# Graph message passing on one core: the sum of the last list of repeated rows stands one item behind the last unit of grouped sums

## The chip, the cores and the metric

The kernel runs on 1 core of one Trainium2 chip. The metric is the device time of one execution in microseconds (us). Before the change the median of 3 runs is 1887.07 us, with runs from 1877.03 to 1892.61.

## The reference, cut to what matters

There are 6250 nodes with 128 features and 200000 edges. Each edge takes the row of its `dst` node (normalised, through a ReLU and a matrix), multiplies it by a filter made from its 20 edge features, and adds the product to the row of its `src` node. The sums go through a small network and are added to `x`.

```python
idx_i, idx_j = pair_indices[0], pair_indices[1]          # src, dst; dst is sorted, src is random
x = atomic_embedding @ W_in                              # atomic_embedding = relu(layernorm(x))
W_ij = shifted_softplus(f_ij @ W_f1 + b_f1) @ W_f2 + b_f2
W_ij = W_ij * f_ij_cutoff
x_ij = x[idx_j] * W_ij
out = jax.ops.segment_sum(x_ij, idx_i, num_segments=N_ATOMS)
return shifted_softplus(out @ W_o1 + b_o1) @ W_o2 + b_o2  # and x + this
```

The part that matters here is `segment_sum`: 200000 rows of 128 numbers, each to be added to one of 6250 rows.

## The kernel before, in words

**Items.** The edges are cut into chunks of 128 and into 391 quads of four chunks. One loop (`for i in range(...)` near the end of the main block) runs over items `i`; at item `i` quad `i` is begun, and quads `i-1` to `i-4` are in later stages. Around these stages the loop runs hooks: `at(i, point, fn, ...)` registers a function for an item and a point in it, and `put(name, i, fn, ...)` does the same with the offset and the point that the table `AT` gives for a name. The points of an item are run in the order L, D0, D1, PE0, ..., A0, A1, AX, DM, DR, PE1, PE2, A2, D2, S. The whole loop is written under a manual schedule, so that each engine's instructions stand in the order in which the loop calls them. Nothing waits for an item as such: every engine runs on through its own queue until an instruction waits for data or for a free buffer.

**Three ways for a row to reach its sum.** The rows of an edge are added in one of three ways, by quad.

- *Plain* quads (the first 12 of those that are not grouped, and quad 390): rows of one chunk with the same `src` are summed by a matrix of equal ids (`s3_pe`), then scattered.
- *Listed* quads (184 of them, in 12 lists of at most 16 quads): the rows are scattered as they are. A scatter (`scatter`, L644) is an indirect DMA that GpSimd issues; it adds 128 rows to one of four accumulators in DRAM, `acc0` to `acc3`, in turn. A row whose `src` has occurred already within its chunk is sent to a row of the list's own region at the end of the accumulators, 128 rows per list. When a list is complete, `l_load` (L513) brings its region from all four accumulators into `lm`; `l_dg`, `over_row` (L807) and `l_same` (L525) compare the ids of its 128 rows with each other; `l_sum` (L531, L532) adds rows of equal id by matmul, over the four copies; `l_copy` (L537), `l_ji` (L542, L543) and `over_int` (L834) make the rows and their indices; and `over_scatter` scatters them into the nodes' rows.
- *Grouped* quads (194: every second one, from 2 to 388): their rows are sorted into slots of node groups by matmul (`permute`) and moved into `mst` by DMA (`regroup`). Eight quads (ten in the last round) make a round, and each round has four *units* of grouped sums. A unit (`unit_pe`, L863) is 96 matmuls, 120 in the last round, into four PSUM tiles `un`, against one-hot matrices that DVE builds (`unit_oh`, L845); `unit_evac` (L879) adds the four tiles to the accumulator `accT` in SBUF. Rows for which a group has no slot left are the *overflow*: for each pair of quads they are summed by `over_row`, `over_eq`, `over_sum` (L818 to L820), `over_copy`, `over_ji` (L830) and `over_int` and are scattered too.

**The end of the loop.** `unit_slots` puts the last round's units at items 395, 397, 399 and 401 (units 0 to 3 in what follows); each eviction stands at the point DM of the next item. The last quad's scatters stand at 394, and so does the overflow of quad 384; that of quad 388 has its sum at 396, its copy at 397, its indices at 398 and 399 and its scatter at 399. The loads of `x` for the output (L1202, L1207) stand at 395 to 399 on SyncE, and DVE adds a bias to them (L1212) at 398 to 407.

**The last list.** For list `w` the code takes the item `i` behind its last quad at which no unit stands: `clear(n, units)` counts `n` up until it is not an item of `units`. The last list ends with quad 389 and has a lag of 5, so that `i` is 394. From it follow: `l_start`, `l_dg` (ScalarE) and `over_row` (TensorE) at 394; `l_same` (DVE) at 395; `l_sum` at the first item from 395 without a unit, 396, at the point PE1, so between unit 0 (395) and unit 1 (397); `l_load` (SyncE) at 395; `l_copy` and `l_ji` at 397; `over_int` and the scatter at 400. The loads of a list wait for the scatters of listed rows, since these may write into its region.

**Buffers that this touches.** `un`, the overflow's sum and row, and the list's row and sum share the PSUM tag "B" with four buffers. The copies of overflow sums and list sums share the tag `os` with six buffers; a buffer is free again when its scatter has been done.

**After the loop.** The scalars of a check (L1418 to L1436) decide whether a slow second pass is needed; it isn't here, but the loop around it makes all engines meet at L1436, when the accumulators' scatters have landed and `accT` is complete. Then the *tail* loads the accumulators (`t_load`, L1521), adds them to `accT`, runs the two output layers and writes the result. `acc0` is read early; the tail reads the other three.

Of the kernel before, what the change touches and what calls it, by code (L numbers as in the profile page):

```python
# [75 lines left out]
def tile_gnn(ctx: ExitStack, tc: tile.TileContext, x, fB, cT, srcT, srcr, srci, dstr, win_, wf1, wf2, bias, bo1c, wo1,  # L76
# [28 lines left out]
    uslots = unit_slots(rounds)  # L105
    units = {i for us in uslots for i in us}
# [13 lines left out]
    NW = -(-(LE - LB) // SW)  # L120
# [3 lines left out]
    wend = [splain[LB + SW * w + wsize[w] - 1] for w in range(NW)]  # L124
    wlag = [LLAG] * (NW - 1) + [LASTLAG]
# [801 lines left out]
    with tc.manual_schedule():  # L927
# [126 lines left out]
        def at(i, point, fn, *a):  # L1054
            hooks.setdefault((i, point), []).append((fn, a))

        def put(name, base, fn, *a, busy=()):
            d, point = AT[name]
            i = max(clear(base + d, busy) if busy else base + d, 0)
            at(i, point, fn, *a)  # L1060
            return i
# [6 lines left out]
        if CE < EP // P:  # L1068
            w = (CE + 4 * NS) // 2
# [169 lines left out]
        for g in range(len(tgroups)):  # L1239
            i = clear(max(r0_at + 1, ret_at + 12), units)  # L1240
# [4 lines left out]
        for r in range(-(-len(mpq) // RKQ)):  # L1245
            i = mpq[RKQ * r]
            early = i < 8
            i = max(i, 4)
# [13 lines left out]
        for w in range(NW):  # L1262
            for g in range(wsize[w] // 4):
                n = LB + SW * (w - 1) + 4 * g - LSHIFT
                i = splain[n] + 2 if w else 6 + 2 * g
                while w and (i not in mpi or i in units):
                    i -= 1
                for k in range(2):
                    kk = (LB + SW * w + 4 * g) // 2 + k
                    at(max(0, i + k - 2), "L", sb_load, kk)  # L1270
                    put("l_eq", i + k, l_eq, kk)
                i = put("l_count", i, l_count, (LB + SW * w) // 4 + g, busy=units)
                k = put("l_dup", i, l_dup, w, g)
            i = put("l_scan", i, l_scan, w)
            i = put("l_before", i - 1, l_before, w, busy=units)
            put("l_index", i, l_index, w)
            assert i + 1 <= splain[LB + SW * w] + 1
            put("l_id", i, l_id, w)
            i = put("l_place", i, l_place, w, busy=units)
            put("l_take", i, l_take, w)  # L1280
            i = clear(wend[w] + wlag[w], units)
            at(i, "L", l_start, w)
            put("l_dg", i, l_dg, w)
            at(i, "PE2", over_row, ("L", w))
            put("l_same", i, l_same, w)
            k = clear(i + AT["l_sum"][0], units)
            at(k - 1, "L", l_load, w)
            at(k, AT["l_sum"][1], l_sum, w)
            put("l_copy", k, l_copy, w)
            put("l_ji", k, l_ji, w)  # L1290
            k = put("l_int", k, over_int, ("L", w))
            at(k, "S", over_scatter, ("L", w))
# [344 lines left out]
def unit_slots(rounds):  # L1637
    end = rounds[-1][-1]
    grouped = {q for qs in rounds for q in qs}
    out, used = [], set()  # L1640
    for r, qs in enumerate(rounds):
        a = qs[-1] + ULAG
        last = r == len(rounds) - 1
        step = 2 if last else min(RND // 2, (rounds[r + 1][-1] - qs[-1]) / 4)
        us = []
        for s in range(4):
            i = a + int(s * step)
            while i in used or (not last and i <= end and not UCLASSES[UCLASS](i, grouped)):
                i += 1
            used.add(i)  # L1650
            us.append(i)
        out.append(us)
    return out
# [10 lines left out]
def clear(i, busy, n=1):  # L1664
    while any(i + k in busy for k in range(n)):
        i += 1
    return i
# [114 lines left out]
```

## Time and profile before

| | us |
|---|---|
| median of 3 runs | 1887.07 |
| lowest and highest run | 1877.03, 1892.61 |
| the profiled execution | 1900.09 |
| its span, first to last instruction | 1898.3 |
| granted TensorE clock, mean over the span | 0.963 |
| unit 0 to unit 3 of the last round, in the trace | 1786.42 to 1845.91 |
| first load of the tail | 1849.09 |

The profile is one execution on the chip. PE is TensorE's matmul, PEld its weight load, DVE is VectorE, ACT is ScalarE, POOL is GpSimd, SP is SyncE; a "q" behind the name is the engine's sequencer or DMA queue. A timeline row has start, duration, engine, line, operation, output and inputs, how many instructions were merged, and in brackets the idle time before it with what ended it. A wait row has who waited, for what, the total, the number of times and the longest. A row of a stretch (A:B) has its length, then busy time and number of instructions of PE, PEld, DVE, ACT and POOL, the granted clock, the DMA engines' share and GB/s. Groups by line end with busy time, mean ns of one, and the idle time before them.

### The profile page before, as it was taken

Reading aid. Unit: us, or ns where it says so; the run is one execution under the profiler, and the core shown is the slowest. Engines: PE = TensorE matmul, PEld = TensorE weight load, DVE = VectorE, ACT = ScalarE, POOL = GpSimd, SP = SyncE. Lnnn points to the kernel's source line nnn. Section 1 sums busy time; section 2 is a strip of 40 time slices with the busy share of each in tenths; the row PEclk is TensorE's granted clock in tenths of the full one; section 3 lists DMA queues with packets and bytes.
Section 4 is the critical chain, followed back from the end, with each engine's and each line's share of the span. In section 5 each row is a group of like instructions: output and inputs, shape, how many; then the busy total and the mean of one; then the engine's idle time right before and its main releaser. Section 6 shows DMA issues by size and latency. Waiting matters only on the chain. (4 is left out here: it accounts for less than half of the span.)

```text
span 1898.3 us, 55497 instructions
## 1 busy us (share of the span) xinstructions
PE 1681.0 (89%) x19308; PEld 1122.6 (59%) x19308; DVE 1605.7 (85%) x4740; ACT 1471.1 (77%) x4068; POOL 1494.5 (79%) x949
## 2 busy tenths in 40 slices
PE   3769989999999999999999999999999999999746
PEld 2546655666666666666665566666666666666524
DVE  6678989899899989898899789889889899888636
ACT  4568878888788888887787788888888888888405
POOL 5557777888888888888888888888888888887845
PEclk8789999999999999999999999999999999999978
DMA  8878988888888888887887888888888888888647
GB/s 301 225 183 194 206 185 172 172 174 182 164 180 168 172 181 168 170 187 162 173 188 154 172 186 173 176 177 166 187 170 174 189 173 175 157 159 188 127 82 267
DMA packets 365471, 339.68 MB, mean 179 GB/s; under 512 B 86686, under 2 KB 328781, under 8 KB 365187
## 3 DMA queue, kind: packets, MB, share of 16 engines
q1 hardware_dynamic: 234005, 270.57, 49.1%
q0 software_dynamic: 130624, 65.33, 33.0%
q8 instruction: 152, 2.49, 0.6%
q14 instruction: 132, 1.08, 0.2%
q10 hardware_dynamic: 558, 0.20, 0.0%
HBM read 150.76 MB, written 108.08 MB: 136 GB/s over the span
## 5 line engine op out<-in xcount | busy, mean ns | idle before, releaser
L644 POOL DMA_INDIRECT acc<-s,lji x736 | 1188.0, 1614 | 245.1 <-issue 178.0
L572 ACT ACTIVATE xc<-xg,cb 128x128 f32<-128x128 f32 x1564 | 445.6, 371 | 16.9 <-PE xg L559 11.5
L567 PEld LDWEIGHTS W<-w,a 128*128 128x128 f32 x3128 | 428.7, 198 | 38.0 <-issue 24.7
L863 PE MATMUL un<-so,mst 32*128 32x392 bf16 x9312 | 433.9, 327 | 9.8 <-ACT sg L766 3.4
L567 PE MATMUL W<-w,a 128*128 128x128 f32 x3128 | 428.0, 281 | 0.1
L766 ACT CAST sg<-pq 128x388 bf16<-128x388 f32 x776 | 345.7, 493 | 84.6 <-DMA mst<-sg 45.4
L758 PE MATMUL pq<-pt,pm 128*128 128x388 bf16 x1552 | 333.4, 338 | 33.2 <-issue 9.1
L863 PEld LDWEIGHTS <-mst 32*128 32x128 bf16 x9312 | 232.8, 93 | 159.6 <-issue 19.0
L384 ACT ACTIVATE a<-a,con 128x512 f32<-128x512 f32 x391 | 282.4, 722 | 11.6
L379 ACT ACTIVATE a<-z 128x512 f32<-128x512 f32 x391 | 241.3, 617 | 39.1 <-PE z L374 34.1
L746 DVE TENSOR_TENSOR pt<-pt 128x512 f32<-128x512 f32 x388 | 264.1, 681 | 0.0
L879 DVE TENSOR_TENSOR accT<-un,accT 128x392 f32<-128x392 f32 x368 | 182.3, 557 | 68.0 <-PE z L374 42.5
L758 PEld LDWEIGHTS <-pm 128*128 128x128 bf16 x1552 | 147.3, 97 | 148.0 <-issue 58.0
L845 DVE TENSOR_SCALAR so<-iot,mst 128x392 bf16<-128x392 f16 x776 | 220.1, 334 | 8.6 <-PE un L863 7.1
L644 POOL DMA_INDIRECT acc<-os,oji x109 | 174.6, 1602 | 45.4 <-issue 17.0
L732 DVE TENSOR_SCALAR pm<-iotp,pos 128x384 bf16<-128x384 f16 x776 | 204.3, 324 | 0.0
L374 PE MATMUL z<-ft,ws 123*128 123x512 bf16 x391 | 155.0, 397 | 38.8 <-DMA ft<-fsd 11.1
L582 DVE TENSOR_TENSOR s<-W,xc 128x512 f32<-128x512 f32 x184 | 125.9, 684 | 70.7 <-issue 39.0
L582 DVE TENSOR_TENSOR pt<-W,xc 128x512 f32<-128x512 f32 x194 | 132.5, 683 | 47.4 <-ACT xc L572 31.0
L559 PE MATMUL xg<-wn,oh 63*128 63x128 bf16 x1564 | 157.1, 222 | 15.0 <-DVE oh L391 11.4
L556 PE MATMUL W<-b2rep,onesb 64*128 64x512 bf16 x391 | 154.5, 395 | 0.0
L781 PE MATMUL po<-pt,pm 128*128 128x387 bf16 x776 | 152.8, 338 | 1.3 <-DVE pt L746 0.7
(214 smaller groups left out, 1845.1 us busy)
## 6 DMA issues: line engine op xcount, KB each, us to landing
mst<-sg SPq DMA_DIRECT2D x776, 97.0 KB
sb<-src SPq DMA_DIRECT2D x98, 256.0 KB
rb<-reld SPq DMA_DIRECT2D x194, 128.0 KB
fsd<-f SPq DMA_DIRECT2D x49, 480.0 KB
ft<-fsd SPq DMA_DIRECT2D x96, 240.0 KB
fb<-in_fB_dram SPq DMA_DIRECT2D x49, 320.0 KB
ft<-fsd SPq DMA_DIRECT2D x96, 160.0 KB
acc<-s,lji POOLq DMA_INDIRECT x736
```

What stands on the lines that cost most here:

```text
L379: nc.scalar.activation(a, st[q]["z"], AF.Exp)
L384: nc.scalar.activation(a, a, AF.Ln, bias=half, scale=0.5)
L567: nc.tensor.matmul(W[:, c, :], st[q]["a"][:, c * P:(c + 1) * P], w2, start=False, stop=(c == 3))
L572: nc.scalar.mul(xc[:, c, :], st[q]["xg"][:, c, :], late["c", q // CQ][:, 4 * (q % CQ) + c:4 * (q % CQ) + c + 1])
L582: nc.vector.tensor_tensor(m[:, :, :P], st[q]["W"], st[q]["xc"], op=ALU.mult)
L644: nc.gpsimd.indirect_dma_start(out=accs[k][:rows, :], out_offset=bass.IndirectOffsetOnAxis(ap=ji, axis=0), in_=s, in_offset=None, compute_ ...
L732: nc.vector.tensor_scalar(pm[:, c], iotp, rk[r]["pos"][:, 4 * j + c:4 * j + c + 1], None, op0=ALU.is_equal)
L746: nc.vector.tensor_tensor(pt[:, :, k * P:(k + 1) * P], a, high(a), op=ALU.subtract)
L758: nc.tensor.matmul(t[:, :MW], mp[q]["pm"][:, c, s * P:(s + 1) * P], high(mp[q]["pt"][:, c:c + 1, :MW])[:, 0], start=(c == 2 * h), stop=(c ...
L766: nc.scalar.copy(mp[q]["sg", h][:, s], mp[q].pop(("q", k))[:, :MW])
L845: nc.vector.tensor_scalar(so, iotw[:, :GN], w[:, 3 * P // 2:3 * P // 2 + 1], None, op0=ALU.is_equal)
L863: nc.tensor.matmul(ts[g][:, :GN], mp[q]["ms", s // 2][v, s % 2, k * P:(k + 1) * P], mp[q]["oh"][v], start=(q == qs[0] and k == 0), stop=(q ...
```

## The change

The item at which the last list's operations start must lie behind the last unit of the last round as well. For all other lists the added term is 0 and nothing changes.

```diff
@@ -1278,7 +1278,7 @@
             put("l_id", i, l_id, w)
             i = put("l_place", i, l_place, w, busy=units)
             put("l_take", i, l_take, w)
-            i = clear(wend[w] + wlag[w], units)
+            i = clear(max(wend[w] + wlag[w], uslots[-1][-1] + 1 if w == NW - 1 else 0), units)
             at(i, "L", l_start, w)
             put("l_dg", i, l_dg, w)
             at(i, "PE2", over_row, ("L", w))
```

With `uslots[-1][-1]` = 401 the item `i` of the last list is 402 instead of 394. `l_start`, `l_dg` and `over_row` stand at 402; `l_load` at 402; `l_same` and `l_sum` at 403; `l_copy` and `l_ji` at 404; `over_int` and the scatter at 407. The loop runs to item 412 as before, and the number and order of the scatters are the same.

## The prediction

> **What bounds the kernel now.** The page came first: TensorE is busy for 89% of the span. The change touches only the end, so next came the waits there (TensorE's from 1790 to 1862 us, SyncE's from 1780) and then the timeline of each engine.
>
> ```profile
> span 1898.3 us, 55497 instructions
> PE 1681.0 (89%) x19308; PEld 1122.6 (59%) x19308; DVE 1605.7 (85%) x4740; ACT 1471.1 (77%) x4068; POOL 1494.5 (79%) x949
> ```
> ```profile
> PE lsum L531 <- DMA lm<-acc: 23.3, 1, 23.3
> ```
> ```profile
> SPq L513 <- DMA acc<-s,lji: 28.1, 1, 28.1
> SPq L1436 <- DVEq L1436: 14.0, 1, 14.0
> ```
>
> TensorE stands still once for 23.3 us, at the sum of the last list (L531), because its rows `lm` have not been loaded. They have not been loaded because SyncE held the load for 28.1 us until the last scatter into the list's rows (`s,lji`) had landed. TensorE's own timeline shows what is queued behind that sum:
>
> ```profile
> 1796.36 0.49 PE L531 MATMUL lsum<-lm,leq 128*128 128x128 f32 x2 [0.83 <-DVE accT L879]
> 1820.12 1.74 PE L531 MATMUL lsum<-lm,leq 128*128 128x128 f32 x6 [23.27 <-DMA lm<-acc]
> ...
> 1822.35 7.17 PE L863 MATMUL un<-so,mst 32*128 32x392 bf16 x120
> 1830.62 0.32 PE L863 MATMUL un<-so,mst 32*128 32x392 bf16 x1 [1.10 <-DVE accT L879]
> ...
> 1839.36 0.32 PE L863 MATMUL un<-so,mst 32*128 32x392 bf16 x1 [0.51 <-DVE accT L879]
> ...
> 1840.78 5.13 PE L863 MATMUL un<-so,mst 32*128 32x392 bf16 x117 [0.15 <-DVE accT L879]
> ```
>
> Three units of grouped sums follow the sum, from 1822.35 to 1845.91 (1840.78 + 5.13): 23.6 us of work that needs nothing of the list. GpSimd meanwhile works off a queue of scatters:
>
> ```profile
> 1798.08 1.54 POOL L644 DMA_INDIRECT acc<-os,oji  x1 [0.30 <-issue]
> ...
> 1807.31 1.54 POOL L644 DMA_INDIRECT acc<-os,oji  x1 [0.30 <-issue]
> ...
> 1814.69 1.54 POOL L644 DMA_INDIRECT acc<-s,lji  x1 [0.30 <-DMA acc<-s,lji]
> 1816.54 1.54 POOL L644 DMA_INDIRECT acc<-os,oji  x1 [0.30 <-issue]
> ...
> 1823.93 1.54 POOL L644 DMA_INDIRECT acc<-os,oji  x1 [0.30 <-issue]
> 1828.62 1.54 POOL L644 DMA_INDIRECT acc<-os,oji  x1 [3.15 <-ACT oji L834]
> 1830.47 1.54 POOL L644 DMA_INDIRECT acc<-os,oji  x1 [0.30 <-POOLq L1436]
> ```
>
> The last scatter is the list's own (1830.47), the one before it that of overflow 388. GpSimd ends at 1832.01, 14 us ahead of TensorE. The tail starts at the point where all engines meet (L1436); SyncE's 14.0 us there wait for DVE, and DVE for the last unit:
>
> ```profile
> 1845.80 1.98 DVE L879 TENSOR_TENSOR accT<-un,accT 128x392 f32<-128x392 f32 x4 [2.95 <-PE un L863]
> 1847.70 0.68 DVE L1212 TENSOR_TENSOR xl<-xl,bo2b 128x512 f32<-128x512 f32 x1
> ```
> ```profile
> 1848.56 0.02 SPq L1436
> ...
> 1849.09 0.38 SPq L1521
> ```
>
> So this stretch is bound by TensorE's queue, delayed by GpSimd's. The tail's first load leaves at 1849.09, and 49.2 us later the span ends; I take the tail as unchanged and forecast that one time.
>
> **The change part by part.** Work is neither added nor dropped. The last list's items move from 394 to 402 (start, diagonal, row), 395 to 402 or 403 (loads, comparison), 396 to 403 (sum), 397 to 404 (copy, index) and 400 to 407 (integer index, scatter). They move past units 1 to 3 on TensorE, their evictions on DVE, overflow 388's steps, and on SyncE past the loads of x, seven of which stood behind the held load. The order on GpSimd stays as it was: 388, then the list.
>
> *What goes from the old place.* DVE's evictions of units 0 and 1, and the list's index between them:
>
> ```profile
> 1795.74 1.98 DVE L879 TENSOR_TENSOR accT<-un,accT 128x392 f32<-128x392 f32 x4 [1.50 <-PE un L863]
> ...
> 1822.41 0.22 DVE L543 SCALAR_TENSOR_TENSOR ojd<-os,con,ojd 128x1 f32<-128x1 f32 x1 [23.64 <-issue]
> ...
> 1830.00 1.98 DVE L879 TENSOR_TENSOR accT<-un,accT 128x392 f32<-128x392 f32 x4 [1.98 <-PE un L863]
> ```
>
> Overflow 388's sum takes the list's place on TensorE at about 1796.4, and unit 1 starts when the eviction of unit 0 (1795.74) has freed its tiles. Unit 2 started 0.6 us after its predecessor's eviction began (1830.62 after 1830.00); with 388's tile to fill first I allow 1.3, so unit 1 starts at 1797.0 instead of 1822.35, 25.35 us earlier. DVE, which the list's index held for 23.6 us, is let go too. With the 23.56 us that the units took, unit 3 would end at 1820.6. The moved loads of x cost nothing on the path: their rows are read by DVE's additions (L1212) only beside or after the units.
>
> *What comes at the new place.* Behind unit 3 stands a chain that nothing covers on TensorE and DVE: eviction 1.98, one addition 0.68 and the comparison 0.34 (to 1823.5), the sum, copy, index, integer index. The prices are in these rows of the earlier lists and of this one:
>
> ```profile
> 1756.27 1.06 PE L531 MATMUL lsum<-lm,leq 128*128 128x128 f32 x8
> 1757.16 0.28 PE L532 MATMUL lsum<-con,leq 128*128 128x1 f32 x2
> ```
> ```profile
> L525 DVE TENSOR_SCALAR leq<-orow,idl x12: 332/343/348, 350.5 to 1788.3; 128x128 f32<-128x128 f32 x12
> ```
> ```profile
> L537 ACT COPY os<-lsum x12: 268/268/269, 356.1 to 1822.1; 128x129 f32<-128x129 f32 x12
> ```
> ```profile
> L834 ACT ACTIVATE oji<-ojd,con x109: 278/305/312, 122.5 to 1828.3; 128x1 int32<-128x1 f32 x109
> ```
>
> The sum takes 1.3 us at that rate, or 2.4 at the rate of the held one (six in 1.74, and four more); copy, index and integer index are 0.27 + 0.22 + 0.31, and I allow 0.1 for each of four handovers. The scatter could be issued at 1826.0 (1827.2 with the slow sum). The diagonal (ScalarE) and the row stand ahead of the comparison and are hidden by the eviction and the addition. The loads don't hold the sum:
>
> ```profile
> 1817.98 1.29 SPq L513 DMA_DIRECT2D lm<-acc  x3
> ```
>
> They went 1.75 us after the last scatter into the list's rows had ended (1814.69 + 1.54), with their data there by 1820.12, and GpSimd's queue up to that scatter is the same now; the sum asks for them at 1823.5.
>
> *What is late next.* GpSimd. From 1798.08 the list's scatter is 16 periods away. In the quiet stretch above a period is (1823.93 - 1798.08) / 14 = 1.846 us, which gives 1827.6. Beside a full DVE it is longer. Over 200 to 1780 us the two rows below make (1150.1 + 235.2 + 159.0 + 37.6) / 811 = 1.951 us, which gives 1829.3:
>
> ```profile
> L644 POOL DMA_INDIRECT acc<-s,lji x712 | 1150.1, 1615 | 235.2 <-issue 172.5 <-DMA acc<-s,lji 21.8 <-DVE accT L879 6.5
> L644 POOL DMA_INDIRECT acc<-os,oji x99 | 159.0, 1606 | 37.6 <-issue 15.8 <-ACT a L379 6.7 <-DMA acc<-s,lji 2.9
> ```
>
> The units load DVE less than the loop and more than the idle stretch, so I take the middle, 1828.5. That is 2.5 us after the chain is ready: **GpSimd's queue ends last**. The scatter runs to 1830.0. In the profile SyncE had everything but DVE's sign at 1848.56 - 14.0 = 1834.6, 2.6 us after the last scatter's end (its landing is in this); and from the last sign to the load are 0.53. The load leaves at 1830.0 + 2.6 + 0.5 = 1833.2 instead of 1849.09. DVE's remaining additions, seven of 0.68 or less, fit between its index near 1825.6 and 1832.6. **The sum is -15.9 us**; the bounds on GpSimd's rate alone make it -16.8 to -15.1.
>
> The profiled execution took 1900.09 us with its span of 1898.3; the runs' median is 13.0 us shorter and even the slowest run 7.5. I take the difference over: span 1882.4, and 1887.07 - 15.9 = **1871.2 us**.
>
> **The rivals.**
>
> *TensorE's side ends last.* It decides once unit 3 ends after 1823.1. For it speaks that a clock of 0.76 to 0.80 was granted in the first two, against 1.00 in the third (the figure behind TensorE's, DVE's, ScalarE's and GpSimd's busy time):
>
> ```profile
> 1822.30:1830.00 7.70, 7.22 (x122) 3.99 (x121) 2.28 (x8) 0.82 (x4) 4.24 (x3) 0.76 1.06 294
> 1830.60:1839.00 8.40, 7.77 (x120) 4.50 (x120) 5.44 (x16) 0.00 (x0) 1.41 (x1) 0.80 0.19 21
> 1839.40:1846.00 6.60, 6.05 (x120) 3.64 (x119) 3.65 (x10) 0.00 (x0) 0.00 (x0) 1.00 0.01 2
> ```
>
> Against it: each started behind a gap, and not all need to. Three units at unit 2's 8.74 us (1830.62 to 1839.36) end at 1823.2; with the slow sum the scatter goes at 1829.8, and the gain is 14.6. As far bound, all three wholly at half clock take twice 5.13 us and 1.5 of start each, end near 1832.3, and leave 5.5 us of gain. Middle of the two: 1877.
>
> *Each scatter stands still while DVE builds a one-hot.* A unit has ten of these:
>
> ```profile
> 1790.11 0.32 DVE L845 TENSOR_SCALAR so<-iot,mst 128x392 bf16<-128x392 f16 x1 [1.23 <-PE un L863]
> ```
>
> Thirty of 0.32 us, all of it lost, are 9.6 us, so the gain falls by 8.7 to 7.2: 1879.9. In unit 0, where both ran together, GpSimd's four periods took 8.12 us instead of 7.38, so 0.7 was lost of the 3.2 of ten one-hots:
>
> ```profile
> 1788.12 1.54 POOL L644 DMA_INDIRECT acc<-s,lji  x1 [0.30 <-issue]
> 1790.70 1.54 POOL L644 DMA_INDIRECT acc<-s,lji  x1 [1.03 <-DVE so L845]
> ...
> 1796.24 1.54 POOL L644 DMA_INDIRECT acc<-s,lji  x1 [0.30 <-issue]
> ```
>
> The Trainium skill speaks for this rival and against the change: "SBUF — State Buffer", section "Who interferes with whom", says that a two-port vector operation, which a tensor_scalar can be, and a GpSimd operation exclude each other for their whole length. By that rule every overlap costs, and the sum would be 1879.9; the trace agrees with about a fifth of that price.
>
> *The queue is shorter in the runs that were timed.* The profiled execution is 13.0 us longer than the median. If all of that were queue on GpSimd, the old load would leave at 1836.1, the new one with TensorE's chain at 1826.0 + 4.7 = 1830.7: a gain of 5.4, 1881.7. Against it: nothing shows that those 13 us lie on GpSimd.
>
> *The stall stays, and the chain is added (slower).* Unit 1's fourth tile is free only when overflow 388's sum has been copied into `os`, one of six buffers that scatters free. If that buffer were the one of 1823.93, landing 1.75 after its end at about 1827.2, the units would end near 1851, the chain and the meeting would add 10 us, and the load would leave 12 us later than now: 1899. Against it: at 1797 four such scatters are queued (1798.08, 1807.31, 1816.54, 1823.93), with 388 five, and there are six buffers. It decides from a queue of six.
>
> **How the numbers follow.** Forecast 0.56; TensorE last 0.16; scatters blocked 0.10; shorter queue 0.14; stall stays 0.04. A difference of 1%, 18.9 us, is about what a measurement of this kernel can tell from no change; its three runs lie 15.6 us apart. The forecast is 3.0 us short of that line (1868.2), and with a spread of some 6 us on a difference of medians about two fifths of its 0.56 fall beyond, 0.07 of the rest: faster 0.30, slower 0.04, same 0.66. The forecast's own bounds are 1870.3 to 1872.0; with the spread of medians and the rivals down to 1881.7 the range is 1862 to 1883.
>
> **What would show it.** Right: L531's wait of 23.3 us gone; unit 1 starting near 1797 and unit 3 ending near 1820.6 on this trace's scale; GpSimd's scatters without a gap from 1798 to the list's at 1828.5; the tail's first load some 3 us after that scatter's end, and SyncE's wait at L1436 ended by GpSimd's last landing and not by DVE. Wrong: a new wait ahead of unit 1, GpSimd idle before its last scatter (TensorE's side was last), scatters spaced by more than 2.0 us during the units, or a tail longer than 49 us.

## The result and the profile after

| | before | after |
|---|---|---|
| median of 10 runs each, us | 1885.57 | 1870.72 |
| lowest and highest run, us | 1877.03, 1892.61 | 1863.87, 1882.14 |
| the profiled execution, its span, us | 1900.09, 1898.3 | 1882.14, 1880.3 |
| first load of the tail, us | 1849.09 | 1830.85 |

The ratio of the medians is 0.9931, 95% interval 0.9905 to 0.9957, so the change took off 0.4 to 1.0%. The first two lines of the page after:

```profile
span 1880.3 us, 55505 instructions
PE 1670.5 (89%) x19308; PEld 1119.6 (60%) x19308; DVE 1612.1 (86%) x4740; ACT 1467.9 (78%) x4068; POOL 1493.7 (79%) x949
```

The averages hardly moved; the end did. The waits of TensorE, SyncE, VectorE and GpSimd between 1772 and 1845 us, after the change:

```profile
PE lsum L531 <- DMA lm<-acc: 12.4, 1, 12.4
...
SPq L513 <- DMA acc<-s,lji: 34.1, 1, 34.1
SPq L1436 <- DMA acc<-os,oji: 10.1, 2, 6.6
...
DVE ojd L543 <- ACT os L537: 15.0, 1, 15.0
POOL acc L644 <- DVE ojd L830: 3.4, 1, 3.4
```

The wait for the list's rows has not gone. SyncE holds the loads even longer (34.1 us instead of 28.1) and TensorE still stands at the sum for 12.4 us. What has changed is who stands behind it. TensorE's timeline:

```profile
1783.41 5.13 PE L863 MATMUL un<-so,mst 32*128 32x392 bf16 x117
...
1790.47 5.13 PE L863 MATMUL un<-so,mst 32*128 32x392 bf16 x117
...
1797.53 5.13 PE L863 MATMUL un<-so,mst 32*128 32x392 bf16 x117 [0.15 <-DVE accT L879]
1803.26 0.46 PE L807 MATMUL orow<-ldg,onesf 128*128 128x128 f32 x2 [0.60 <-DVE accT L879]
1805.45 0.80 PE L531 MATMUL lsum<-lm,leq 128*128 128x128 f32 x2 [1.73 <-DVE leq L525]
1818.66 1.87 PE L531 MATMUL lsum<-lm,leq 128*128 128x128 f32 x6 [12.42 <-DMA lm<-acc]
```

Units 1 to 3 end at 1797.53 + 5.13 = 1802.66, ahead of the wait. GpSimd's timeline, first the overflow scatter behind which 18 scatters stand up to the last listed one, then the places where it lost time, then the end:

```profile
1774.00 1.54 POOL L644 DMA_INDIRECT acc<-os,oji  x1 [0.30 <-DMA acc<-s,lji]
1775.85 1.54 POOL L644 DMA_INDIRECT acc<-s,lji  x1 [0.30 <-issue]
1778.52 1.54 POOL L644 DMA_INDIRECT acc<-s,lji  x1 [1.13 <-DMA acc<-s,lji]
...
1787.38 1.54 POOL L644 DMA_INDIRECT acc<-s,lji  x1 [3.42 <-DVE ojd L830]
...
1791.07 2.88 POOL L644 DMA_INDIRECT acc<-s,lji  x1 [0.30 <-issue]
...
1796.11 1.54 POOL L644 DMA_INDIRECT acc<-os,oji  x1 [0.30 <-issue]
...
1813.25 1.54 POOL L644 DMA_INDIRECT acc<-s,lji  x1 [0.30 <-DMA acc<-s,lji]
...
1824.83 1.54 POOL L644 DMA_INDIRECT acc<-os,oji  x1 [0.31 <-issue]
1826.67 1.54 POOL L644 DMA_INDIRECT acc<-os,oji  x1 [0.30 <-DMA acc<-os,oji]
```

The list's index is ready, and the tail starts, by these rows of ScalarE and of SyncE:

```profile
1821.34 0.29 ACT L834 ACTIVATE oji<-ojd,con 128x1 int32<-128x1 f32 x1 [0.29 <-DVE ojd L543]
```
```profile
1830.85 19.38 SPq L1521 DMA_DIRECT2D ta_in<-acc  x30
```

The list's scatter could have gone at 1821.63 and went at 1826.67, behind a queue without a gap; the tail's load follows 2.64 us after its end. GpSimd's queue ended last.

**Three yardsticks** serve below, since two executions of one kernel differ by several us. *D* runs from the start of the last listed scatter (`s,lji`) to the tail's first load. *A* runs from the overflow scatter ahead of 18 scatters (here 1774.00) to that same listed scatter, so it is GpSimd's pace; at the 1.846 us of the quiet stretch it would be 33.2. *Q* is the number of scatters that GpSimd has still to start up to the end when VectorE's eviction of unit 0 begins. Before: D = 1849.09 - 1814.69 = 34.40, and A = 1814.69 - 1780.74 = 33.95 by the row below; after: D = 1830.85 - 1813.25 = 17.60, A = 1813.25 - 1774.00 = 39.25. Q was 18 and 22.

```profile
1780.74 1.54 POOL L644 DMA_INDIRECT acc<-os,oji  x1 [0.30 <-ACT oji L834]
```

### The profile page after: what moved, and what is told of

The parts are those of the page before. It is cut to its first block, busy times and chain, and to the rows that moved or that the text cites. A ratio compares the mean times of both kernels' runs of the same rounds, so it can differ in the third digit from the quotient of the medians.

```text
span 1880.3 us, 55505 instructions
## 1 busy us (share of the span) xinstructions
PE 1670.5 (89%) x19308; PEld 1119.6 (60%) x19308; DVE 1612.1 (86%) x4740; ACT 1467.9 (78%) x4068; POOL 1493.7 (79%) x949
## 4 chain that ended last, share of the span: by engine, by line
PE 39%; DVE 27%; DMA 12%; ACT 11%; issue 5%; POOL 4%; SPq 2%; DVEq 0%; ACTq 0%; POOLq 0%
PE un L863 10%; PE W L567 8%; PE pq L758 6%; DMA mst<-sg 5%; PE po L781 4%; DMA acc<-s,lji 4%; ACT sg L766 4%; DVE accT L879 3%; POOL acc L644 3%; DVE pt L746 3%; PE z L374 3%; DVE pm L732 3%; ACT xc L572 3%; DVE s L582 2%; DVE so L845 2%
## 5 line engine op out<-in xcount | busy, mean ns | idle before, releaser
L567 PEld LDWEIGHTS W<-w,a 128*128 128x128 f32 x3128 | 427.4, 198 | 41.6 <-issue 28.1
L732 DVE TENSOR_SCALAR pm<-iotp,pos 128x384 bf16<-128x384 f16 x776 | 208.1, 328 | 0.0
```

The source lines that it names most:

```text
L567: nc.tensor.matmul(W[:, c, :], st[q]["a"][:, c * P:(c + 1) * P], w2, start=False, stop=(c == 3))
L732: nc.vector.tensor_scalar(pm[:, c], iotp, rk[r]["pos"][:, 4 * j + c:4 * j + c + 1], None, op0=ALU.is_equal)
```

## The experiments

The theory: the gain is the work that no longer queues behind the held sum, and after the change GpSimd's queue ends last. Its rivals: TensorE's side ends last; the one-hots of the units hold GpSimd up; the loads of `x`, let go early, hold GpSimd up.

| run | edit, in short | median us | ratio to before, 95% interval | D | A | Q |
|---|---|---|---|---|---|---|
| e1 | sum behind unit 1 | 1879.21 | 0.9964 (0.9941 to 0.9987) | 24.98 | 36.4 | 21 |
| e2 | sum behind unit 2 | 1875.83 | 0.9946 (0.9925 to 0.9966) | 17.06 | 36.5 | 18 |
| e3 | after, three scatters fewer | 1869.61 | 0.9908 (0.9876 to 0.9941) | 13.14 | 35.7 | 18 |
| e4 | before, three scatters fewer | 1886.45 | 1.0007 (0.9985 to 1.0030) | 31.95 | 33.6 | 17 |
| e5 | after without the loads of `x` | 1893.15 | 0.9941 (0.9916 to 0.9966) | 30.0 | 33.3 | 10 |
| e6 | after, loads of `x` spread out | 1894.13 | 0.9956 (0.9931 to 0.9981) | 29.5 | 34.2 | 10 |
| e7 | after, one-hots in another form | 1897.97 | 0.9965 (0.9944 to 0.9985) | 25.9 | 37.8 | 12 |
| e8 | e6 and e7 together | 1899.33 | 0.9970 (0.9947 to 0.9994) | 31.2 | 36.2 | 10 |
| e9 | after, once more | 1883.06 | 0.9912 (0.9882 to 0.9943) | 22.2 | 37.7 | 14 |
| e10 | before, once more, a single run | 1892.08 | none | 33.2 | 34.1 | 14 |
| e11 | e5 once more | 1888.40 | 0.9943 (0.9919 to 0.9967) | 23.7 | 34.2 | 13 |
| e12 | e2 once more | 1883.45 | 0.9917 (0.9892 to 0.9941) | 17.61 | 38.9 | 14 |

Runs e1 to e4, e5 to e8 and e9 to e12 each shared a chip and an occasion (the first and the third group the same chip), and before on the same occasion had medians of 1885.26, 1904.30 and 1899.99. In e3 and e4 the queue itself is three scatters shorter, so that their Q of 18 and 17 stand for 21 and 20. Times are compared within such a group, and between groups by ratios only.

### Where the sum stands: e1 and e2

```diff
-            i = clear(wend[w] + wlag[w], units)
+            i = 396 if w == NW - 1 else clear(wend[w] + wlag[w], units)
```

That is e1: the sum falls between units 1 and 2, with two units queued behind it. In e2 the number is 398: one unit behind it.

> The last list starts at item 396, so its sum stands between units 1 and 2. Yardstick: D, from the start of the last scatter into the list's rows to the tail's first load (34.4 us before, 17.6 us after the change). Theory (the held sum costs what is queued behind it on TensorE, and behind all units GpSimd's queue ends last): two units stay behind the sum, so D is 7.7 to the first unit's start, some 15 for two units and 3.2 to the load, about 26, and the time lies some 8 us above the changed kernel's, near 1879. Rival (the gain comes from DVE and TensorE being let go at once, wherever behind unit 0 the sum stands): D near 17.6 and the changed kernel's time.

> The last list starts at item 398, so its sum stands between units 2 and 3. Theory: one unit of 7 to 8 us stays behind the sum; D is 7.7 + 7.5 + 3.2, about 18.4, within 1.5 us of the changed kernel's 17.6, because GpSimd's last scatters run beside that unit: time like the changed kernel's. Rival (in the changed kernel the list's own chain behind the last unit sets the end): without that chain at the end the time falls by 5 us or more.

TensorE's wait in e1, and the rows of its timeline behind it:

```profile
PE lsum L531 <- DMA lm<-acc: 20.8, 1, 20.8
```
```profile
1804.50 1.77 PE L531 MATMUL lsum<-lm,leq 128*128 128x128 f32 x6 [20.84 <-DMA lm<-acc]
...
1806.41 7.34 PE L863 MATMUL un<-so,mst 32*128 32x392 bf16 x120
```

The wait is nearly as long as before (20.8 us against 23.3), yet D falls from 34.40 to 24.98 because two units stand behind it and not three: they took 14.4 us here, the three of before 23.56. In e2 the wait is 8.4 us, one unit stands behind it, and D is 17.06, the same as after:

```profile
1818.54 1.67 PE L531 MATMUL lsum<-lm,leq 128*128 128x128 f32 x6 [8.44 <-DMA lm<-acc]
1820.37 6.54 PE L863 MATMUL un<-so,mst 32*128 32x392 bf16 x120
```

So the length of the wait is not the price; what is queued behind it is, until GpSimd's own end (D near 17) is reached. With one unit behind the sum that floor is already reached. The medians go the same way: 1879.21 in e1, where 1879 was expected, and 1875.83 in e2, whose interval overlaps that of after.

### Is GpSimd last: e3 and e4

Both leave out the three scatters of quad 390, which stand between the last listed scatter and the list's own (the output lacks those rows); e3 is the kernel after, e4 the one before.

```diff
-            for c in range(nchunks(q)):
+            for c in range(0 if q == NQ - 1 else nchunks(q)):
```

> The changed kernel without the three scatters of quad 390 (the rows of that quad are left out of the sums). They stand in GpSimd's queue behind the last listed scatter. Theory (GpSimd's queue ends last): D falls by the room that the list's chain leaves, from 17.6 to about 12.9, and the time by 4 to 5 us. Rival (the list's chain or TensorE ends last): D and the time stay.

> The kernel before without the three scatters of quad 390 (the rows of that quad are left out of the sums). Theory (there the held sum and the units behind it set the end, and GpSimd is done 14 us earlier): D stays at 34.4 within 1 us, and the time stays. Rival (GpSimd's whole queue bounds both kernels alike): 4 to 5.5 us less.

In e3 D fell by 17.60 - 13.14 = 4.5 us: three periods of 1.85 are 5.5, less the 1.2 us that GpSimd now stood idle ahead of the list's scatter (1.48 instead of 0.30), which makes 4.3:

```profile
1813.89 1.54 POOL L644 DMA_INDIRECT acc<-s,lji  x1 [0.30 <-DMA acc<-s,lji]
...
1822.45 2.02 POOL L644 DMA_INDIRECT acc<-os,oji  x1 [1.48 <-DVE xl L1212]
```

In e4 the three scatters bought no time: ratio 1.0007. GpSimd only stood idle longer, 8.54 us ahead of its last two scatters, where the profile of before had 3.15:

```profile
1817.37 1.54 POOL L644 DMA_INDIRECT acc<-os,oji  x1 [8.54 <-ACT oji L834]
```

D of e4 was to stay within 1 us and fell by 2.45; its units 2 and 3 ran at 7.06 us each by these rows, as after, where in the profile of before three took 23.56, 7.85 each:

```profile
1809.20 1.65 PE L531 MATMUL lsum<-lm,leq 128*128 128x128 f32 x6 [27.55 <-DMA lm<-acc]
1811.35 6.93 PE L863 MATMUL un<-so,mst 32*128 32x392 bf16 x120
...
1820.19 5.13 PE L863 MATMUL un<-so,mst 32*128 32x392 bf16 x117 [0.15 <-DVE accT L879]
...
1827.25 5.13 PE L863 MATMUL un<-so,mst 32*128 32x392 bf16 x117 [0.15 <-DVE accT L879]
```

So GpSimd's end bound the kernel after and not the one before. In the ratios to before e3 (0.9908) can't be told from after (0.9931), as their intervals overlap: 4.5 us are a quarter of a per cent.

### What slowed GpSimd: e5 to e8

A had risen by 5.3 us with the change. Two things could do that: the loads of `x`, which now go in one burst, and the one-hots, which now run beside the scatters. In e5 all thirteen loads are left out, ten of L1202 and three of L1207 (the output lacks `x`):

```diff
-                nc.sync.dma_start(wide(xl[g][:, :T], T), rows(x, o, T))
...
-            nc.sync.dma_start(wide(xl[g][:, :T], T), rows(x, o, T))
...
-            nc.vector.tensor_tensor(v, v, bo2b.unsqueeze(1).to_broadcast([P, T, P]), op=ALU.add)
+            b = bo2b.unsqueeze(1).to_broadcast([P, T, P])
+            nc.vector.tensor_tensor(v, b, b, op=ALU.add)
```

In e6 they are there, but each tile's loads wait for a small write of VectorE, two items apart:

```diff
+        def x_gate(k):
...
+            nc.vector.memset(late["xl", k][:, 0:1], 0.0)
...
-            at(mpq[-1] + 7 + k, "L", x_load, k)
+            at(mpq[-1] + 6 + 2 * k, "D2", x_gate, k)
+            at(mpq[-1] + 7 + 2 * k, "L", x_load, k)
```

In e7 the last round's one-hots are made by another form of instruction, and e8 is e6 with this form:

```diff
+                nc.vector.scalar_tensor_tensor(so, iotw[:, :GN], w[:, 3 * P // 2:3 * P // 2 + 1],
+                                               onesc.to_broadcast([P, GN]), op0=ALU.is_equal, op1=ALU.mult)
```

> The changed kernel without the ten loads of x at the end (the output lacks x; the thirteen additions stay, of the bias to itself). Yardstick: A, from the overflow scatter eight listed ones ahead of the next overflow scatter to the last listed scatter, 18 periods of GpSimd (33.95 us before, 39.25 us after the change; 33.2 at the quiet 1.846 us). Theory X (the loads, let go early by the change, share the DMA engines with the scatters, whose landings come late, and GpSimd waits for the landing of the scatter into the same accumulator): A falls to 33.5 to 35 us, the time by 3 to 5 us against the changed kernel. Rival L (DVE's one-hots, now beside the scatters, hold GpSimd): A stays at 37 us or more.

> The changed kernel with the loads of x spread over the units: each of the four tiles is first written at one element by DVE, at 394, 396, 398 and 400, and its loads stand an item later (the last tile's three loads at 401). Theory X: fewer scatters meet several loads at once, A 34 to 37 us, the time 1 to 4 us under the changed kernel's. Rival L: A stays near 39 us. If the sum of the transfers counts and not their crowding, A stays too, although X holds.

> The changed kernel with the last round's forty one-hots built by scalar_tensor_tensor (compare, then times one) in place of tensor_scalar, about 0.45 instead of 0.32 us each. Rival L (the two-port form of the one-hots holds GpSimd): no scatter beside a unit is longer than 1.6 us except beside an addition, and A falls by 1.5 us or more, to 37.5 or less. Theory X alone: A within 1 us of 39.25.

> Both edits, spread loads and the other form of one-hots. If both causes hold, A is the lowest of these runs with x loaded, 34 to 36 us, and the time 2 to 5 us under the changed kernel's, about 1867.

As to A: without the loads 33.3, within 0.1 us of the quiet pace; spread out, 34.2; with the other form of one-hot 37.8 and, the loads spread, 36.2. That the loads are the cause and the one-hots in their old form are not rests on e5, and on e11 below. e6 says little of spreading: only five of its thirteen loads left inside A (the first at 1805.00, while A ends at 1816.48), so the others can't have lengthened it. The 37.8 of e7 lies between what the two theories gave (37.5 or less, 38.25 or more), and e8 was not the lowest. The new form was no gain for GpSimd: e8 differs from e6 by it alone and has 36.2 against 34.2, each from one execution. A one-hot took 0.63 us instead of 0.32. The scatters beside them took 1.8 to 1.9 us inside A, and behind it up to twice the usual 1.54, as these in e7:

```profile
1824.92 3.22 POOL L644 DMA_INDIRECT acc<-os,oji  x1 [0.30 <-DMA acc<-s,lji]
1828.44 2.92 POOL L644 DMA_INDIRECT acc<-s,ji  x1 [0.30 <-issue]
```

As to the time these four did not answer, and none reached the ratio of after (0.9931), though the intervals overlap. Q was 10 to 12 here, so GpSimd was through early and waited for the list's index; a faster GpSimd could bring nothing. GpSimd's longest wait in e5 and in e6:

```profile
POOL acc L644 <- ACT oji L834: 12.8, 1, 12.8
```
```profile
POOL acc L644 <- DVE xl L1217: 12.0, 1, 12.0
```

### Once more on one chip: e9 to e12

The kernel after, the kernel before, e5 and e2, unchanged, side by side.

> The changed kernel once more, on the chip of the next three. Let Q be the scatters that GpSimd has still to start when the eviction of unit 0 begins: 18 in the profile of before, 22 in that of after, 10 to 12 in those of the last four runs, where the list's own scatter started 8 us and more after GpSimd had nothing left to do. Theory: with Q of 18 or more GpSimd's queue ends last, its scatters follow without a gap and D is 17.6 within 1.5 us; with Q near 10 the list's chain behind unit 3 ends last, GpSimd idles ahead of the last scatter and D is near 30. Rival: the idle GpSimd of the last four runs came from their edits, and D is 17.6 here whatever Q is.

> The kernel before once more, for its profile on this chip. Theory: TensorE's wait at the last list's sum follows Q, some 23 us at 18 and (18 - 10) * 1.85 = 15 us less, about 8, at 10; D stays 32 to 35 either way, because what stands behind the sum stays. The gain of the change on a chip with Q near 10 is then the wait of 8 us less the chain, near 5, and not 15. Rival (the gain doesn't depend on the queue): a wait of 20 us or more whatever Q is.

> The changed kernel without the loads of x (the output lacks x; the additions stay, of the bias to itself), beside the changed kernel on one chip. Theory X (the loads delay the scatters' landings): A lies 2 to 6 us under the changed kernel's of this chip, near 33.5, and with Q of 18 or more the time lies 2 to 5 us lower; with Q near 10 the time stays within 2 us, because GpSimd doesn't end last. Rival L (DVE's one-hots hold GpSimd): A within 1 us of the changed kernel's.

> The list's sum between units 2 and 3, beside the changed kernel on one chip. Theory: with Q of 18 or more like the changed kernel within 2 us; with Q near 10 the list's chain (comparison, sum, copy, indices, scatter and its landing, some 10 us) runs beside unit 3 instead of behind it, and the time is 3 to 6 us lower than the changed kernel's. Rival (the place behind the last unit is the best one in any state): 2 us or more slower than the changed kernel.

A with the loads (e9) was 37.7, without them (e11) 34.2: 3.5 us on one occasion, as the theory has it. Single executions differ, as after, e3 and e9 run the same instructions in A and have 39.25, 35.7 and 37.7. Still, the seven profiles of the table and of after with the whole burst, or most of it, inside A have 35.7 to 39.25 (after, e1, e2, e3, e7, e9, e12), and the six with no loads or at most five there 33.3 to 34.2 (before, e4, e5, e6, e10, e11). GpSimd's losses in e9 stand again beside and just behind the burst of ten loads, which left from 1798.77:

```profile
1808.00 1.54 POOL L644 DMA_INDIRECT acc<-s,lji  x1 [1.28 <-DMA acc<-s,lji]
1811.41 1.64 POOL L644 DMA_INDIRECT acc<-s,lji  x1 [1.87 <-DMA acc<-os,oji]
...
1834.27 1.54 POOL L644 DMA_INDIRECT acc<-os,oji  x1 [0.30 <-DMA acc<-s,ji]
1840.88 2.01 POOL L644 DMA_INDIRECT acc<-os,oji  x1 [5.07 <-DVE xl L1212]
```

The last row shows another end than in the first profile after, though not the expected D near 30 (22.2): Q was 14, GpSimd stood idle for 5.07 us ahead of the list's scatter, and the chain behind unit 3 was last. The rival, 17.6 whatever Q is, fell with it. In e12, where the sum does not wait for unit 3, GpSimd had no gap there and D was 17.61, 4.6 less than in e9 (SyncE waited another 0.6 us for VectorE's sign, so unit 3 itself was last); but the medians are 1883.45 and 1883.06, so these 4.6 us of two single executions do not show in the time, which was expected 3 to 6 us lower. Nor does e11's faster GpSimd: its 1888.40 are 5.3 us above e9, where 2 at most were expected, with intervals that overlap.

The shorter queue shows in before as well. In e10 the wait at the sum was 15.8 us:

```profile
PE lsum L531 <- DMA lm<-acc: 15.8, 1, 15.8
```

Four scatters fewer in the queue than in the first profile of before are 4 x 1.85 = 7.4 us less of the 23.3, which gives 15.9. So the change should bring less on this occasion. From the eviction of unit 0 to the tail's first load the profiles of e10 and e9 have 44.8 and 36.0 us, 8.8 apart. The medians, though, are 1899.99 - 1883.06 = 16.9 us apart. The profiled executions of e9 and e10 took 1897.74 and 1892.08 us, 14.7 above and 7.9 below their kernels' medians on this occasion, so they need not be typical. Why the gain did not shrink stays open.

## Why the prediction was right, point by point

*The time.* Forecast 1871.2, measured 1870.72. The forecast took off 15.9 us from 1887.07; the medians of ten runs differ by 14.85, with an interval of 8 to 18 us. The span fell by 18.0, but 6.74 of that (1780.74 - 1774.00) had been gained before the scatter from which A counts, where the order of work is the same; the tail was 49.45 us instead of 49.2. From that scatter to the tail's load it is 68.35 before and 56.85 after: a net gain of 11.5 in the pair of profiles. That forecast and median agree within 0.5 us is therefore partly luck: the mechanism, as the profiles show it, brought 4.4 us less than forecast, the medians lie between the two, and their interval can't tell 11.5 from 15.9.

*"L531's wait of 23.3 us gone": wrong as put.* 12.4 us are left, without harm: behind it stand only additions. The list's rows were to be there before the sum asks for them; they were not, since units 1 to 3 ended 12.1 us ahead of the last listed scatter's end (1802.66 and 1814.79 us), not 4.4 behind it as forecast (1820.6 and 1816.23). There are three reasons. TensorE was ahead of GpSimd already in this execution: Q was 22 and not 18, four scatters or 7.4 us. GpSimd lost some 5 us more behind that point, as told below. And the units were quicker: from 1782.47 to 1802.66 they took 20.2 us, not 23.56. The first row of unit 1:

```profile
1782.47 0.79 PE L863 MATMUL un<-so,mst 32*128 32x392 bf16 x3
```

*"GpSimd's queue ends last": right* where Q is high, shown by e3 against e4 and by the gap-free end. With Q of 10 to 14 (e5, e6, e9, e11) it was the chain behind unit 3. That is the rival "the queue is shorter in the runs that were timed"; its state was met, its small gain (5.4 us) was not.

*"From 1798.08 the list's scatter is 16 periods away", at 30.4 us: right.* The same 16 took 1826.67 - 1796.11 = 30.56. The meeting was 2.64 us from the scatter's end, not 3.1.

*"The moved loads of x cost nothing on the path": the step that failed.* They cost GpSimd. In the nine periods ahead of those 16 it took 1796.11 - 1774.00 = 22.11 us after, 1798.08 - 1780.74 = 17.34 before: 4.77 lost. Of the loss 3.1 are the idle stretch ahead of 1787.38, 0.8 the one ahead of 1778.52, 0.2 two short ones between them and 1.3 the long scatter at 1791.07; before had lost 0.7 there itself. What lengthened that scatter the runs don't show, so that the loads account for some 4 us here and not for all of the loss. The terms close: 15.9 - 4.77 - 0.14 (30.56 for 30.42) + 0.5 (the meeting) = 11.5. Three of the ten loads of L1202 had been ahead of the held load before, and seven behind it; these left from 1819.36 on, when GpSimd had five scatters to go. Now all go at once. SyncE's rows, two of before and one of after:

```profile
1786.52 2.79 SPq L1202 DMA_DIRECT2D xl<-in_x_dram  x3
...
1819.36 3.56 SPq L1202 DMA_DIRECT2D xl<-in_x_dram  x7
```
```profile
1772.56 6.08 SPq L1202 DMA_DIRECT2D xl<-in_x_dram  x10
```

The stretch of the burst after, and then the one before in which three of the loads left (the last two columns are the DMA engines' share and GB/s):

```profile
1774.00:1783.00 9.00, 7.70 (x124) 5.17 (x124) 4.57 (x13) 0.27 (x1) 6.74 (x5) 0.81 1.08 314
```
```profile
1783.00:1790.00 7.00, 3.89 (x37) 2.63 (x39) 4.67 (x16) 2.14 (x8) 5.75 (x4) 0.89 0.77 168
```

With the DMA engines that busy the scatters landed later, and a scatter waits until the third one ahead of it, into the same accumulator, has landed. The landing signals in the trace show both. The six scatters that started from 1772.16 to 1782.42 landed 5.7 to 8.1 us after their start, those of 1787.38 and 1789.23 after 3.3 and 3.2. The row at 1778.52 names such a wait. The row at 1787.38 names VectorE's index `ojd`, but a listed scatter reads no such index: GpSimd's queue stood there for the scatter of 1778.52, which landed at 1786.65, and went on at 1786.67. In e9 the scatters from 1801.01 to 1805.18, beside the burst, took 6.7 to 7.8 us to land; in e11, without the loads, none from 1784 on took more than 4. So the loads are the cause, by A in e5 and e11 and by the landings.

*"TensorE's side ends last": not in the first profile*, as none of units 1 to 3 ran slowly there and Q was high. In e9 units 2 and 3 took 6.81 us for the matmuls that took 5.13 after, and the chain was last, with GpSimd at 5.07 us of idleness.

*"Scatters blocked by one-hots": refuted at its price.* In e11 the units' one-hots run beside the scatters, and these keep the quiet pace:

```profile
1801.90 1.54 POOL L644 DMA_INDIRECT acc<-os,oji  x1 [0.30 <-DMA acc<-s,lji]
...
1829.64 1.54 POOL L644 DMA_INDIRECT acc<-os,oji  x1 [0.30 <-issue]
```

Fifteen periods took 27.74 us, 1.849 each. The Trainium skill's rule in "SBUF — State Buffer", section "Who interferes with whom", that a two-port vector operation and a GpSimd operation exclude each other, has no visible price for these `tensor_scalar` one-hots; the same section's case of a vector operation with two inputs in SBUF holds only against a GpSimd operation that reads SBUF, and whether the scatters of 2.9 to 3.2 us in e7 are that case no run here shows.

*"The stall stays": not seen.* No wait stood ahead of unit 1 in the profile after, although Q was 22.

## What to carry to other kernels

A wait costs what is queued behind it in program order, not its own length: moving a held sum behind work that doesn't need it left 12.4 us of the wait in place and still took off the time. When such a hold goes, list what else it held back: here seven loads, let go nearly 40 us earlier by GpSimd's queue (0.3 us behind the scatter from which A counts, not 38.6), met a stretch full of scatters and gave back some 4 us in the profile after and 3.5 in e9 against e11. And a floor under the gain, here GpSimd's own queue, is found by taking work from that queue in both kernels: it must shorten the one and not the other.

## What was not expected of the hardware

*The clock of the units.* The forecast took the three units at the 23.56 us of before, where the granted clock was 0.76 and 0.80 for the first two. After, units 1 to 3 had 1.00; the stretch of unit 2:

```profile
1790.00:1797.00 7.00, 6.09 (x120) 3.69 (x120) 5.52 (x17) 0.00 (x0) 6.09 (x4) 1.00 0.35 32
```

The idle stretch ahead of them does not decide it. In e4 TensorE had stood still for 27.55 us, and the second and third unit behind that ran at the full rate (5.13 us for 117 matmuls). In e9 TensorE stood still for only 1.1 and 1.0 us ahead of units 2 and 3 (0.5 after), and they were granted 0.81 and 0.80:

```profile
1818.00:1827.00 9.00, 7.54 (x121) 4.49 (x120) 5.65 (x17) 0.00 (x0) 7.48 (x6) 0.81 0.41 37
1827.50:1836.00 8.50, 7.38 (x119) 4.28 (x118) 3.40 (x9) 0.00 (x0) 7.09 (x5) 0.80 0.46 61
```

By the clock records of the trace each of these two means is a single stretch of 3.4 us at half clock (from 1819.2 and from 1829.5), with the full clock around it. What decides when such a stretch comes was not tried.

*Occasions.* The same kernel before had medians of 1885, 1904 and 1900 us on three occasions, of which the first and the third were on one chip, so the chip alone doesn't make the difference. The profiles of the slower two had Q of 10 to 14, those of the first 17 to 22. Which end comes last differs with that, so one profile tells of the occasion on which it was taken. What sets Q was not tried.
